# Seeding an edge-weight bank in the step that frees it, and making the edge weights one step earlier

## The chip, the core and the metric

The kernel runs on one core of a Trainium2 chip. The core has five engines that run side by side, each through its own list of instructions in order: TensorE does matrix products (PE in the profile; its weight loads are listed apart as PEld), VectorE (DVE) and ScalarE (ACT) do elementwise work, GpSimd (POOL) issues the gathers here, and SyncE (SP) issues plain DMA transfers. Engines wait for each other through semaphores. PSUM is the memory that TensorE writes its products to; it has eight banks, and VectorE and ScalarE read and write it too. The metric is the time of one execution on the device in microseconds (us); lower is better.

## What is computed

A graph network with three layers over 6250 nodes and 100000 edges, 256 features wide, and a layer norm at the end. Edges come sorted by destination.

```python
ew = edge_attr @ edge_w + edge_b                  # one weight row of 256 for each edge
for l in range(3):
    msg = relu(x[src] * ew)
    out = 0
    for i in range(3):                            # three types of edge
        h = segment_sum(msg * rel_masks[i][:, None], dst, n)
        out = out + (h * inv_cnt[i][:, None]) @ weights[l, i]
    x = x + relu(out + x @ roots[l] + biases[l])
out = layernorm(x0 + x)
```

The weights `ew` don't depend on the layer, but at 100000 x 256 numbers they are too large to keep, so each layer makes them again.

## The kernel before

Edges are cut into 391 pairs of 128-edge tiles, 256 edges a pair; two pairs are a quad. A layer takes the pairs in a fixed order: pairs 64 to 390 first, then pairs 63 down to 0. So at place p of the order the first pair of a quad stands at an even p up to place 326, and at an odd p after it. (Pair 390 is alone in its quad.)

Everything inside a layer is laid out by hand in a loop over steps `it`, one pair a step. An engine runs its instructions in the order in which this loop writes them down, so the loop is the schedule; nothing reorders it. For a quad whose first pair has place p, the steps before were:

- step p-9 and p-8, `gather`: GpSimd issues two indirect DMA transfers a pair (L989), which bring rows x[src] into `xs`; there are eight such quad buffers. SyncE loads the edge attributes `at` of eight pairs at once, nine steps ahead.
- step p-6, `seed_ew` (L611): ScalarE copies the bias `seed` into two PSUM banks `ew_p`, one for each pair. There are four such banks, so a quad uses those of the quad two before it (place p-4).
- step p-5, `make_ew` (L624): TensorE adds edge_attr @ edge_w onto the bias in these banks. In each layer the first four pairs get their bias from a small product (L620) instead of the seed.
- step p-3, `weigh`: VectorE multiplies bank and gathered rows (L646, once for each pair), ScalarE applies the relu to the quad (L648).
- step p-2, `one_hot` (L654): VectorE makes the matrices that say which node and type an edge belongs to.
- step p and p+1, `reduce`: TensorE sums the messages by node into a PSUM bank `h_p`, of which there are two.

A bank `h_p` serves a span: the pairs that fall into the same 40 nodes. Where edges are dense, a span has several pairs; then `reduce` takes the form of L668, and the span is `turned`: one step after its last pair ScalarE copies the bank out (`take`, L684), TensorE transposes it back (`turn`, L688), and in the step after that VectorE adds it to `acc` (`add`, L704). Where a span is a single pair, `reduce` takes the form of L676 and `add` follows in the next step. A layer has 244 spans, 57 of them turned; at places 77 to 140 all spans are turned spans of two pairs, which open at an odd place and close at the even place after it. From place 141 to 326 every span is one pair.

Between these steps lies the work on nodes: each 128 nodes that are complete go through `node_mul` on TensorE (L732) and `node_end` on VectorE (L763, L766), ScalarE clears their part of `acc` (L749, L752), and `root_turn`, `root_turned`, `root_mul`, `root_keep` (L709, L713, L717, L720) make x @ roots.

Within one step the order is: gathers and loads; `reduce`; `take`; `make_ew`; `turn`; `weigh`; `seed_ew`; the root and node work; `one_hot`; `add`. In the two lines below the loop's `pair(k)` is the pair at place it+k, and `first_of` says that it is the first of its quad:

```python
            if pair(5) is not None and first_of(it + 5, 2):
                make_ew(pair(5) // 2)
```

Up to place 326, `weigh` and `make_ew` therefore fall into odd steps, and `seed_ew` and `one_hot` into even steps; an odd step weighs the quad at place it+3, makes the weights of the quad at it+5, and the even step after it seeds the quad at it+7 counted from the odd step.

Of the kernel before, what the change touches and what calls it, by code (L numbers as in the profile page):

```python
# [442 lines left out]
def ordered_path(ctx, tc, x, attr_laid, A, weights, roots, biases, edge_w, edge_b, out, src, src_i, seg, place_i, consts, x_root,  # L443
# [19 lines left out]
    order, _, moved, least, most = schedule(N, E, 1)  # L463
# [75 lines left out]
    def first_of(p, n):  # L539
        return p == 0 or order[p - 1] // n != order[p] // n  # L540
# [8 lines left out]
    def closes(u):  # L549
        p = order.index(u)  # L550
        return p == U - 1 or span_of[order[p + 1]] != span_of[u]
# [28 lines left out]
    def layer(l, r_sb, b_sb, ats, early, pools):  # L580
# [22 lines left out]
        def pairs_of(q):  # L603
            return range(min(2, U - 2 * q))

        def seed_ew(q):

            for u in range(2 * q, 2 * q + len(pairs_of(q))):
                ew_ps[u] = ew_pool.tile([P, 2, D], F32, name="ew_p")
                if len(ew_ps) > OCT:  # L610
                    nc.scalar.activation(ew_ps[u], seed, AF.Copy)  # L611

        def make_ew(q):

            n = len(pairs_of(q))
            at = ats[2 * q // GROUP][:, q % (GROUP // 2), :]
            done = seen[0]
            seen[0] += n
            for k in range(max(0, min(n, OCT - done))):
                nc.tensor.matmul(ew_ps[2 * q + k].rearrange("p i d -> p (i d)"), full_ones[:PARTS, :],  # L620
                                 bias.rearrange("p i d -> p (i d)"), start=True, stop=False)
            for k in range(n):
                half = slice(k * 2 * A, (k + 1) * 2 * A)
                nc.tensor.matmul(ew_ps[2 * q + k].rearrange("p i d -> p (i d)"), at[half, :],  # L624
                                 ew_sb[half].rearrange("p i d -> p (i d)"), start=False, stop=True,
                                 skip_group_check=done + k >= OCT)
# [16 lines left out]
        def weigh(q, pairs=None):  # L643
            pairs = pairs_of(q) if pairs is None else pairs
            for k in pairs:
                nc.vector.tensor_mul(xs[q][:, k], ew_ps[2 * q + k], xs[q][:, k])  # L646
            there = xs[q][:, pairs.start:pairs.stop]
            nc.scalar.activation(there, there, AF.Relu)  # L648
# [32 lines left out]
        def take(span):  # L681
            n = D + 1 if l == 0 else D
            h_ss[span] = edge.tile([P, D + 1], F32, name="h_s", bufs=2)
            nc.scalar.activation(h_ss[span][:WK, :n], h_ps[span].rearrange("p c w -> p (c w)")[:WK, :n], AF.Copy)  # L684
# [114 lines left out]
        for j, c in enumerate(turns_of):  # L799
            step = max(3 + int((U - 110) * (1 - (1 - j / NT) ** 0.5)), max(root_at, default=-1) + 6)  # L800
            if j >= ROOTS:
                step = max(step, starts[turns_of[j - ROOTS]] + 5)
            assert step + 8 <= starts[c]
            root_at[step] = c
        for it in range(-11, max(starts) + 8):
            def pair(k):
                return order[it + k] if 0 <= it + k < U else None
# [20 lines left out]
                reduce(pair(0))  # L828
            if pair(-1) is not None and closes(pair(-1)) and turned(span_of[pair(-1)]):
                take(span_of[pair(-1)])  # L830
            if pair(5) is not None and first_of(it + 5, 2):
                make_ew(pair(5) // 2)
            if pair(-1) is not None and closes(pair(-1)) and turned(span_of[pair(-1)]):
                turn(span_of[pair(-1)])
            if pair(3) is not None and first_of(it + 3, 2):
# [4 lines left out]

            if pair(3) is not None and pair(3) // 2 == order[-1] // 2:
                weigh(pair(3) // 2, range(pair(3) % 2, pair(3) % 2 + 1))
            if pair(6) is not None and first_of(it + 6, 2):
                seed_ew(pair(6) // 2)
            if it - 6 in root_at:
                root_keep(root_at[it - 6])
            if it in root_at:
# [31 lines left out]
    with tc.manual_schedule():  # L879
        state = (*load_root(0), {}, first_rows)  # L880
        for l in range(L):
            with ExitStack() as pools:
                state = layer(l, *state, pools)
# [12 lines left out]
OCT = 4  # L896
# [25 lines left out]
def turned(span):  # L922

    return span[0] > 0 and span[1] > span[0] + 1
# [234 lines left out]
```

## Time and profile before

| what | value |
|---|---|
| three runs | 3673.85, 3688.68, 3698.54 us; median 3688.68 |
| the profiled execution | 3671.94 us, of it 3670.1 us from the first to the last instruction |
| mean granted TensorE clock | 0.883 of full speed |
| ScalarE busy | 1560.9 us, 43% of the span |
| VectorE busy | 1921.4 us, 52% |
| GpSimd busy | 2238.7 us, 61% |

Rows of the profile have the form "line engine operation out<-in shape xcount | busy us, mean ns of one | idle time of the engine just before them, and what ended it". A row of waits reads "engine, what it was about to do <- what released it: us in total, times, longest". A row of the timeline has the start in us, the length, and in brackets how long the engine stood idle before it and who released it; "x4" means four records merged into one row. One fp32 product of TensorE leaves two records, so a `make_ew` of a quad (two products) is four. The releaser "remote" or "issue" means that the profile doesn't show one.

### The profile page before, as it was taken

What the parts mean: (1) busy time and instruction counts of PE and PEld (TensorE: products, weight loads), DVE (VectorE), ACT (ScalarE), POOL (GpSimd) and SP (SyncE); (2) the same over time, 40 slices, a digit from 0 to 9 for tenths busy, and PEclk for the clock granted to TensorE, in tenths of its full rate; (3) what the DMA queues carried; (4) which work ended last, traced back from release to release, by engine and by line L of the source; (5) the groups of instructions that cost most, each with busy time, mean ns of one, the idle gap of its engine ahead of it and who ended that gap; (6) DMA issues with size and microseconds to landing.
All of it is one profiled execution on the core that took longest, in us unless ns stands there. A gap on an engine that the chain in (4) does not pass through costs nothing.

```text
span 3670.1 us, 44965 instructions
## 1 busy us (share of the span) xinstructions
PE 2851.4 (78%) x13712; PEld 1930.1 (53%) x13712; DVE 1921.4 (52%) x5485; ACT 1560.9 (43%) x2487; POOL 2238.7 (61%) x2355
## 2 busy tenths in 40 slices
PE   4787888788887767777778888776777877878877
PEld 2455565666664534445555665453444555555545
DVE  4444455566654344445555555433455565666654
ACT  3545454455444343444334344333444444434443
POOL 5666666565566566666666666656666666666664
PEclk9889999899898878988899899878788898999987
DMA  4433333333333333333333333333333333333332
GB/s 132 121 111 117 109 109 104 95 104 100 103 106 109 96 94 97 107 99 105 101 103 103 102 106 109 104 107 100 108 104 111 113 106 114 108 110 111 106 106 70
DMA packets 173571, 387.48 MB, mean 106 GB/s; under 512 B 43450, under 2 KB 78924, under 8 KB 173324
## 3 DMA queue, kind: packets, MB, share of 16 engines
q0 software_dynamic: 112608, 307.65, 29.5%
q1 hardware_dynamic: 53136, 68.50, 5.8%
q10 hardware_dynamic: 7580, 8.37, 0.8%
q8 instruction: 115, 1.88, 0.2%
q14 instruction: 132, 1.08, 0.1%
HBM read 364.88 MB, written 19.46 MB: 105 GB/s over the span
## 4 chain that ended last, share of the span: by engine, by line
PE 52%; another core or an unknown queue 15%; issue 12%; DVE 11%; ACT 5%; DMA 2%; POOL 2%; DVEq 1%; ACTq 0%; POOLq 0%; SPq 0%
PE h_p L676 15%; PE ew_p L624 13%; PE h_p L668 9%; PE o_p L732 8%; DVE xs L646 3%; PE r_p L717 3%; DVE acc L704 2%; POOL xs L989 2%; DVE oh L654 2%; ACT ew_p L611 2%; DVE x_root L763 2%; DMA xs<-x_mid,src_io 2%; ACT xs L648 2%; PE h_p L688 1%
## 5 line engine op out<-in xcount | busy, mean ns | idle before, releaser
L989 POOL DMA_INDIRECT xs<-x_mid,src_io x1564 | 1490.2, 953 | 920.3 <-issue 656.8
L648 ACT ACTIVATE xs<-xs 128x1024 f32<-128x1024 f32 (+1 forms) x588 | 616.7, 1049 | 1365.8 <-DVE xs L646 1235.7
L676 PE MATMUL h_p<-oh,xs 128*128 128x120 f32 x5160 | 790.0, 303 | 323.9 <-DVE acc L704 227.7
L989 POOL DMA_INDIRECT xs<-in_x_dram,src_io x770 | 733.8, 953 | 472.0 <-issue 316.1
L676 PEld LDWEIGHTS h_p<-oh,xs 128*128 128x128 f32 x5160 | 709.6, 211 | 519.5 <-DVE acc L704 291.1
L646 DVE TENSOR_TENSOR xs<-ew_p,xs 128x512 f32<-128x512 f32 x1167 | 751.7, 682 | 418.1 <-remote 172.6
L624 PE MATMUL ew_p<-ew_sb,at 64*128 64x512 f32 x2346 | 772.2, 720 | 100.0 <-ACT ew_p L611 73.7
L704 DVE TENSOR_TENSOR acc<-h_p,acc 128x240 f32 (+1 forms) x732 | 326.0, 445 | 996.9 <-remote 320.9
L668 PE MATMUL h_p<-xs,oh 128*120 128x256 f32 x2088 | 622.7, 431 | 151.0 <-DVE acc L704 76.9
L611 ACT ACTIVATE ew_p<-seed 128x512 f32<-128x512 f32 x1161 | 641.6, 586 | 0.0
L668 PEld LDWEIGHTS h_p<-xs,oh 128*120 128x120 f32 x2088 | 384.2, 204 | 317.5 <-issue 145.4
L654 DVE TENSOR_SCALAR oh<-iota_w,seg_o 128x120 f32<-128x120 f32 x2346 | 515.0, 293 | 0.0
L732 PE MATMUL o_p<-w_sb,acc 128*128 128x256 f32 (+1 forms) x1716 | 469.7, 413 | 48.0 <-DVE x_root L763 34.8
L732 PEld LDWEIGHTS o_p<-w_sb,acc 128*128 128x128 f32 (+1 forms) x1716 | 330.6, 205 | 175.8 <-issue 87.3
L624 PEld LDWEIGHTS ew_p<-ew_sb,at 64*128 64x128 f32 x2346 | 211.4, 207 | 239.0 <-issue 111.2
L763 DVE SCALAR_TENSOR_TENSOR x_root<-o_p,inv,x_root 128x256 f32<-128x256 f32 (+1 forms) x429 | 206.1, 480 | 168.0 <-remote 48.7
L684 ACT ACTIVATE h_s<-h_p 120x256 f32<-120x256 f32 (+1 forms) x171 | 65.3, 382 | 460.5 <-remote 259.7
L717 PE MATMUL r_p<-r_sb,t_s 128*128 128x256 f32 x588 | 170.1, 415 | 19.7 <-issue 14.1
L658 ACT ACTIVATE oh_b<-oh 128x480 bf16<-128x480 f32 x196 | 116.3, 593 | 145.5 <-DVE oh L654 112.9
L749 ACT ACTIVATE acc<-zero_o 128x768 f32<-128x768 f32 (+1 forms) x150 | 140.7, 938 | 82.7 <-PE r_p L732 21.8
L688 PEld LDWEIGHTS h_p<-ident_o,h_s 120*128 120x128 f32 x342 | 38.9, 154 | 238.8 <-ACT h_s L684 113.9
L688 PE MATMUL h_p<-ident_o,h_s 120*128 120x120 f32 x342 | 80.1, 320 | 99.3 <-ACT h_s L684 75.9
(103 smaller groups left out, 957.1 us busy)
## 6 DMA issues: line engine op xcount, KB each, us to landing
at<-in_attr_laid_dram SPq DMA_DIRECT2D x147, 256.0 KB
xs<-x_mid,src_io POOLq DMA_INDIRECT x1564
xs<-in_x_dram,src_io POOLq DMA_INDIRECT x770
x_mid<-x_all SPq DMA_DIRECT2D x96, 128.0 KB
x_all<-in_x_dram ACTq DMA_DIRECT2D x8, 768.0 KB
x<-in_x_dram SPq DMA_DIRECT2D x48, 128.0 KB
out_dram<-x_all SPq DMA_DIRECT2D x48, 128.0 KB
w_sb<-in_L_gnn_weights_dram SPq DMA_DIRECT2D x3, 768.0 KB
```

The source lines that it names most:

```text
L611: nc.scalar.activation(ew_ps[u], seed, AF.Copy)
L624: nc.tensor.matmul(ew_ps[2 * q + k].rearrange("p i d -> p (i d)"), at[half, :], ew_sb[half].rearrange("p i d -> p (i d)"), start=False, st ...
L646: nc.vector.tensor_mul(xs[q][:, k], ew_ps[2 * q + k], xs[q][:, k])
L648: nc.scalar.activation(there, there, AF.Relu)
L654: nc.vector.tensor_scalar(ohs[q][:, t, :], iota_w, seg[:, 4 * q + t:4 * q + t + 1], None, op0=ALU.is_equal)
L668: nc.tensor.matmul(by_node[:WK, :D], ohs[u // 2][:, t, :], xs[u // 2][:, u % 2, i, :], start=(i == 0 and opens(u)), stop=(i == 1 and close ...
L676: nc.tensor.matmul(h_ps[span][:, d, :], xs[u // 2][:, u % 2, i, d * P:(d + 1) * P] if d < DC else full_ones, (ohs if d < DC else oh_bs)[u ...
L704: nc.vector.tensor_tensor(there, h_ps[span][:, :CH].rearrange("p c (r w) -> p c r w", r=R), there, op=ALU.add)
L717: nc.tensor.matmul(rs[c][:, 1, :], t_ss[c][:, d, :], r_sb[:, d, :], start=(d == 0), stop=(d == DC - 1))
L732: nc.tensor.matmul(o_p[:n, j, :], acc[:, d, r, slot:slot + n], w_sb[:, r * DC + d, :], start=(d == 0), stop=(d == DC - 1))
L763: nc.vector.scalar_tensor_tensor(root, o_p[:n, j, :], inv[:n, c, r:r + 1], root, op0=ALU.mult, op1=ALU.add)
L989: nc.gpsimd.indirect_dma_start(out=xs[:, u % 2, i, :], out_offset=None, in_=x_rows[:, :], in_offset=bass.IndirectOffsetOnAxis(ap=src_i[:, ...
```

## The change

Seeding is no longer tied to a fixed step ahead of its quad. A table `seed_at` is made before the loop. For each quad it holds the latest of two steps: p-7, and the step in which the quads that used the same banks are weighed. `seed_ew` runs in that step, behind `weigh`; `make_ew` runs in the step after it. For all but two quads of a layer both entries are the same step, p-7, so `seed_ew` moves from step p-6 to p-7 and `make_ew` from p-5 to p-6; `weigh` stays at p-3. For the two quads at places 327 and 329, where the order turns round, seeding stays at p-6 and making at p-5. No instruction is added, removed or changed in shape.

```diff
@@ -802,6 +802,11 @@
                 step = max(step, starts[turns_of[j - ROOTS]] + 5)
             assert step + 8 <= starts[c]
             root_at[step] = c
+        at_first = {u // 2: p for p, u in reversed(list(enumerate(order)))}
+        seed_at = {}
+        for q, p in at_first.items():
+            used = [order[j - OCT] // 2 for j in range(p, p + len(pairs_of(q))) if j >= OCT]
+            seed_at[max([p - 7] + [at_first[x] - 3 for x in used])] = q
         for it in range(-11, max(starts) + 8):
             def pair(k):
                 return order[it + k] if 0 <= it + k < U else None
@@ -828,8 +833,8 @@
                 reduce(pair(0))
             if pair(-1) is not None and closes(pair(-1)) and turned(span_of[pair(-1)]):
                 take(span_of[pair(-1)])
-            if pair(5) is not None and first_of(it + 5, 2):
-                make_ew(pair(5) // 2)
+            if it - 1 in seed_at:
+                make_ew(seed_at[it - 1])
             if pair(-1) is not None and closes(pair(-1)) and turned(span_of[pair(-1)]):
                 turn(span_of[pair(-1)])
             if pair(3) is not None and first_of(it + 3, 2):
@@ -840,8 +845,8 @@
 
             if pair(3) is not None and pair(3) // 2 == order[-1] // 2:
                 weigh(pair(3) // 2, range(pair(3) % 2, pair(3) % 2 + 1))
-            if pair(6) is not None and first_of(it + 6, 2):
-                seed_ew(pair(6) // 2)
+            if it in seed_at:
+                seed_ew(seed_at[it])
             if it - 6 in root_at:
                 root_keep(root_at[it - 6])
             if it in root_at:
```

On each engine the order of instructions therefore moves like this. TensorE: up to place 326 `make_ew` leaves the odd steps, where it stood between `reduce` and `turn`, for the even steps, where it stands behind `reduce` too. ScalarE: the two copies of a quad stand directly behind the relu of the quad whose banks they take, ahead of that step's other copies and clears, and no longer behind the `take` of the next step. VectorE, GpSimd and SyncE keep their order.

## The prediction

> **What bounds the kernel now.** I read the page first, then the waits, then the groups with their shapes kept apart, then the timeline of two places where TensorE stands still.
>
> ```profile
> span 3670.1 us, 44965 instructions
> PE 2851.4 (78%) x13712; PEld 1930.1 (53%) x13712; DVE 1921.4 (52%) x5485; ACT 1560.9 (43%) x2487; POOL 2238.7 (61%) x2355
> ```
>
> TensorE is the busiest engine, and it stands still for 3670.1 - 2851.4 = 819 us. No other engine comes near the span. So a change of order can only win from these 819 us, and only where it gives TensorE work in a gap. The waits say what ends the gaps:
>
> ```profile
> PE h_p L676 <- DVE acc L704: 227.7, 123, 6.8
> PE h_p L668 <- DVE acc L704: 76.9, 24, 6.3
> PE h_p L688 <- ACT h_s L684: 75.9, 31, 6.4
> PE ew_p L624 <- ACT ew_p L611: 73.7, 14, 17.6
> PE ew_p L624 <- DMA at<-in_attr_laid_dram: 5.0, 1, 5.0
> DVE xs L646 <- PE ew_p L624: 120.4, 83, 7.1
> ACT h_s L684 <- remote: 259.7, 48, 13.1
> ```
>
> The largest item is a reduce that opens a span and waits until VectorE has added the span two before it, because there are two h_p banks. `make_ew` itself waits for the seeds of ScalarE for 73.7 us, in 14 places; VectorE's weighing waits for `make_ew` for 120.4 us.
>
> **The change, part by part.** The prices:
>
> ```profile
> L676 PE MATMUL h_p<-oh,xs 128*128 128x120 f32 x5160 | 790.0, 303 | 323.9 <-DVE acc L704 227.7 <-issue 83.2 <-DVE oh L654 5.9
> L611 ACT ACTIVATE ew_p<-seed 128x512 f32<-128x512 f32 x1161 | 641.6, 586 | 0.0
> L648 ACT ACTIVATE xs<-xs 128x1024 f32<-128x1024 f32 x579 | 611.1, 1055 | 1353.8 <-DVE xs L646 1224.0 <-issue 121.9 <-DMA xs<-x_mid,src_io 3.9
> ```
>
> All instructions stay, so busy time stays; only order counts.
>
> *The stage of two-pair spans.* Here the opening reduce stands at an odd place, and before the change the odd step also holds `make_ew`, behind it. So `make_ew` stands on the wrong side of the gap:
>
> ```profile
> 1506.48 1.13 PE L624 MATMUL ew_p<-ew_sb,at 64*128 64x512 f32 x4
> 1507.54 1.12 PE L668 MATMUL h_p<-xs,oh 128*120 128x256 f32 x4
> 1510.66 1.06 ACT L648 ACTIVATE xs<-xs 128x1024 f32<-128x1024 f32 x1 [5.65 <-DVE xs L646]
> 1511.62 1.10 ACT L611 ACTIVATE ew_p<-seed 128x512 f32<-128x512 f32 x2
> 1513.60 0.41 DVE L704 TENSOR_TENSOR acc<-h_p,acc 128x240 f32 x1 [2.98 <-remote]
> 1514.07 2.06 PE L668 MATMUL h_p<-xs,oh 128*120 128x256 f32 x4 [5.40 <-DVE acc L704]
> 1516.06 2.08 PE L624 MATMUL ew_p<-ew_sb,at 64*128 64x512 f32 x4
> 1518.07 0.66 PE L688 MATMUL h_p<-ident_o,h_s 120*128 120x120 f32 x2
> ```
>
> TensorE ends the even step's reduce at 1508.66, stands still for 5.40 us until the add, reduces, and then spends 2.08 us in `make_ew`. The seeds for it were ready at 1511.62 + 1.10 = 1512.72. After the change the `make_ew` comes directly behind the reduce of 1507.54, so it runs inside the gap, and the add, the reduce and the `turn` keep their times. What is saved is one `make_ew`, 1.13 us at full speed. The `turn` loses nothing by this: before, a reduce and a `make_ew` lie between the last product of the span and its `turn`, after it a `make_ew` and a reduce. How often this happens, by the windows of the stage in the three layers (280 to 485, 1508 to 1709, 2717 to 2913 us), each with its group of reduces and its two rows of waits:
>
> ```profile
> L668 PE MATMUL h_p<-xs,oh 128*120 128x256 f32 x260 | 82.0, 441 | 23.6 <-issue 18.6 <-DVE acc L704 5.0
> PE h_p L668 <- issue: 18.6, 5, 7.8
> PE h_p L668 <- DVE acc L704: 5.0, 4, 3.7
> L668 PE MATMUL h_p<-xs,oh 128*120 128x256 f32 x260 | 70.9, 407 | 32.4 <-issue 23.0 <-DVE acc L704 9.1
> PE h_p L668 <- issue: 23.0, 8, 6.9
> PE h_p L668 <- DVE acc L704: 9.1, 3, 5.4
> L668 PE MATMUL h_p<-xs,oh 128*120 128x256 f32 x260 | 75.2, 425 | 27.6 <-issue 14.7 <-DVE acc L704 12.9
> PE h_p L668 <- issue: 14.7, 6, 5.0
> PE h_p L668 <- DVE acc L704: 12.9, 5, 5.5
> ```
>
> That is 23.6 + 32.4 + 27.6 = 83.6 us in 9 + 11 + 11 = 31 gaps, and the step that waits for a bank is the opening one. A gap can hide one `make_ew`: at most 31 x 1.13 = 35 us. A few gaps are shorter than that, so I take 0.9 each: 28 us won, between 0 and 35.
>
> The Trainium skill bears on the size of this (TensorE: Matmul & The Clock Gate, Part 1): it says that TensorE's clock falls to half after an idle window of about 3.4 us, and returns after as long a busy one. The rows above agree: behind the gap of 5.40 us a reduce takes 2.06 and a `make_ew` 2.08 us, where they take 1.12 and 1.13 before it. By that rule a `make_ew` that leaves the place behind a gap that long saves 2.08 - 1.13 = 0.95 us more; if a third of the 31 gaps are that long (an estimate), the 28 us would be 38. I leave that out.
>
> *The stage of one-pair spans.* Its gaps are the 323.9 us of L676, on which I take nothing. A reduce at place p+2 waits for the add of place p, which waits for the reduce of place p. Between the two reduces lie exactly one odd and one even remainder of a step, so exactly one `make_ew`, before and after. It only moves within the same window:
>
> ```profile
> 2201.07 1.94 PE L676 MATMUL h_p<-oh,xs 128*128 128x120 f32 x16
> 2202.94 1.13 PE L624 MATMUL ew_p<-ew_sb,at 64*128 64x512 f32 x4
> 2203.99 1.13 PE L732 MATMUL o_p<-w_sb,acc 128*128 128x256 f32 x4
> 2207.82 0.41 DVE L704 TENSOR_TENSOR acc<-h_p,acc 128x240 f32 x1 [4.58 <-remote]
> 2208.28 3.67 PE L676 MATMUL h_p<-oh,xs 128*128 128x120 f32 x16 [3.16 <-DVE acc L704]
> ```
>
> Here the gap of 3.16 us stands behind two reduces, a `make_ew` and node work; after the change the `make_ew` stands between the two reduces instead of behind them, and the gap begins and ends where it did.
>
> *Weighing earlier.* VectorE no longer waits for the `make_ew` just in front, at most the 120.4 us. That is worth something only where the add behind it is waited for: 123 + 24 = 147 gaps of TensorE against the 732 adds (three layers of 244 spans) are a fifth, 24 us; and in most of the 83 waits VectorE would go on to wait for the reduce behind that `make_ew`. I take 10, between 0 and 24.
>
> *The seeds.* ScalarE's 1161 copies of 586 ns keep their number. They lose the `take` and the clears ahead of them, and put their 1.17 us a quad ahead of `t_s` and of the clears, for which nobody waits soon. But `make_ew` now needs them one step of TensorE earlier, and everything on TensorE behind it waits too. Where `make_ew` already waits for them, 14 times, the next step's reduce used to run first and now runs after: 14 x 0.97 us (a reduce of eight records, half of the sixteen at 2201.07) = 14 us lost. Most of this lies where one layer ends and the next begins, as the waits of one such stretch, 2270 to 2540 us, show:
>
> ```profile
> PE ew_p L624 <- ACT ew_p L611: 32.6, 6, 17.6
> ```
>
> There the lower bound is 0, if what feeds the stretch sets its pace anyway. New waits of this kind are the second rival, below.
>
> *The loads.* `at` is loaded in step p-9 and now read in step p-6 instead of p-5, so it has three steps to land where it had four. TensorE waited for it once in the whole trace, for 5.0 us. Nothing in SyncE's and GpSimd's queues is moved past anything else; a gather waits for a buffer that a reduce sets free, and the reduces hardly move. Zero; if the one wait came once a layer, 15 us.
>
> Sum: -28 - 10 + 14 = -24 us against 3671.94 (the span and 1.84 us around it), so 3648. The median of the runs shown lies 3688.68 - 3671.94 = 17 us higher, and the runs spread over 25; against the median it is 3665.
>
> **The rivals.** *Gaps of all stages are filled.* If half of the waits at L676 (123 for the add alone) stand ahead of an even step's work as in the first timeline, and nothing is lost at the other half, some 62 gaps more hide 1.13 us each, 70 us, and the earlier weighing brings its 24: 3688.68 - 28 - 70 - 24 + 14 = 3581. For it speaks that VectorE's lateness has many causes; against it, that a gap at an even place loses the cover that a gap at an odd place gains.
>
> *The new wait for the seeds.* This one ends slower. `make_ew` stands one reduce behind the point where VectorE's weighing begins the chain relu, copy: 1.06 + 0.59 = 1.65 us after the weighing ends. In the first timeline it has them 1512.72 - 1508.66 = 4.06 us late, inside a gap; where there is no gap and the add that lets TensorE reduce comes directly behind the weighing, TensorE has only that add's 0.41 and the reduce's 0.97 to cover 1.65, so it stops, and any further delay on ScalarE is added in full. ScalarE is held in 48 places by a `take` that waits for long (259.7 us, 5.4 each), and the relu and seeds queue behind that `take`. The Trainium skill speaks for this rival (PSUM — Partial Sum Buffer, Engine vs sequencer instructions): ScalarE's queue is strictly first in, first out, and TensorE's products keep program order, so a reduce that is ready can't pass a `make_ew` that isn't. The 14 waits agree. If one quad in four (147 of the 588 of three layers) loses 0.68 us (1.65 less one reduce), that is 100 us; with the sum above 3688.68 - 24 + 100 = 3765. It decides from 24 / 0.68 = 35 such quads on. Against it: in most quads the weighing runs well ahead, since VectorE and ScalarE are busy for only 52% and 43%.
>
> *Nothing happens.* TensorE arrives earlier at a gap that something unseen ends ("remote", "issue"), and the change moves idle time about: 3689.
>
> **How the numbers follow.** The forecast, a small gain, has 0.42: its own range is -59 (35 + 24, nothing lost) to 0, so 3630 to 3689. All gaps filled 0.18; new waits 0.3; nothing 0.1. About 1%, 37 us, is what a measurement of this kernel can tell from no change. Faster by more than that: 0.16 of the forecast's 0.42 and the whole of the second case, 0.34. Slower: most of the third case, 0.24. Within: 0.42, from the rest. The range leaves out the better half of the second case and the worse half of the third: 3590 to 3740.
>
> **What would show it.** Right: in the same stage the idle time ahead of L668 falls from 83.6 to about 55 us, the idle time ahead of L676 stays near 324, "DVE xs <- PE ew_p" falls from 120.4 to a quarter, and "PE ew_p <- ACT ew_p" grows by some 14 us. Wrong on the fast side: L676 loses idle time too. Wrong on the slow side: `make_ew` waits for the seeds in a hundred places or more instead of 14. PE's busy time should stay within 1 or 2%, by the granted clock.

## The result, and the profile after

The changed kernel takes 3717.6 us (median of 7 runs, 3711.9 to 3725.9), the kernel before 3684.5 us (7 runs, the three above among them, 3673.9 to 3698.5). The ratio is 1.0099, with a 95% interval of 1.0080 to 1.0118: a loss of 33 us, 1%, where 24 us less than before were forecast. The profiled execution of the changed kernel took 3712.46 us, with a granted clock of 0.884 (0.883 before). The ratios here and below leave out executions that fell into a slower state; among the runs of this document these are two of the six of e4, its profiled one among them.

From the page of the changed kernel, its span, TensorE's totals and the groups that the prediction spoke of (busy us, mean ns of one | idle us just ahead of them, and what ended most of it):

```profile
span 3710.7 us, 45116 instructions
PE 2921.6 (79%) x13712; PEld 1970.6 (53%) x13712; DVE 1912.7 (52%) x5485; ACT 1564.1 (42%) x2487; POOL 2240.9 (60%) x2355
L676 PE MATMUL h_p<-oh,xs 128*128 128x120 f32 x5160 | 793.0, 303 | 304.2 <-DVE acc L704 213.6
L624 PE MATMUL ew_p<-ew_sb,at 64*128 64x512 f32 x2346 | 813.7, 720 | 127.2 <-ACT ew_p L611 81.5
L668 PE MATMUL h_p<-xs,oh 128*120 128x256 f32 x2088 | 630.5, 433 | 85.6 <-DVE acc L704 61.7
L704 DVE TENSOR_TENSOR acc<-h_p,acc 128x240 f32 (+1 forms) x732 | 325.2, 444 | 1148.7 <-issue 360.8
L688 PE MATMUL h_p<-ident_o,h_s 120*128 120x120 f32 x342 | 77.9, 314 | 133.0 <-ACT h_s L684 100.8
```

The same groups of the kernel before, from its page:

```profile
L624 PE MATMUL ew_p<-ew_sb,at 64*128 64x512 f32 x2346 | 772.2, 720 | 100.0 <-ACT ew_p L611 73.7
L704 DVE TENSOR_TENSOR acc<-h_p,acc 128x240 f32 (+1 forms) x732 | 326.0, 445 | 996.9 <-remote 320.9
L668 PE MATMUL h_p<-xs,oh 128*120 128x256 f32 x2088 | 622.7, 431 | 151.0 <-DVE acc L704 76.9
L688 PE MATMUL h_p<-ident_o,h_s 120*128 120x120 f32 x342 | 80.1, 320 | 99.3 <-ACT h_s L684 75.9
```

The gaps ahead of the reduces did shrink, by 65 us at L668 (151.0 to 85.6) and by 20 us at L676 (323.9 to 304.2). TensorE's idle time in all fell by only 30 us, though (819 to 789), and its busy time grew by 70 us. The odd item is `make_ew` (L624): the same 2346 records with the same mean of 720 ns are busy for 41.5 us longer. The busy time of a line is the time in which at least one of its instructions runs. So the same instructions run side by side less often.

The waits say why. First the changed kernel's, then three rows of the kernel before (time, number of waits, the longest):

```profile
PEld ew_p L624 <- ACT ew_p L611: 121.5, 112, 15.6
PE ew_p L624 <- ACT ew_p L611: 81.5, 26, 15.2
DVE xs L646 <- PE ew_p L624: 52.7, 30, 6.8
```

```profile
PEld ew_p L624 <- ACT ew_p L611: 81.3, 25, 18.0
PE ew_p L624 <- ACT ew_p L611: 73.7, 14, 17.6
DVE xs L646 <- PE ew_p L624: 120.4, 83, 7.1
```

The matmuls wait for the copies hardly longer than before (73.7 to 81.5 us), but their weight loads (PEld) now wait in 112 places instead of 25. (The traces of these two executions hold some 18,000 semaphore updates each, where those of e1 and e5 hold 53,000, so the counts of waits are likely too low in both.) One such place in the timeline of the changed kernel (start, length, engine, line):

```profile
1352.87 1.06 ACT L648 ACTIVATE xs<-xs 128x1024 f32<-128x1024 f32 x1 [4.50 <-issue]
1353.83 1.10 ACT L611 ACTIVATE ew_p<-seed 128x512 f32<-128x512 f32 x2
1354.46 0.29 PEld L624 LDWEIGHTS ew_p<-ew_sb,at 64*128 64x128 f32 x2 [2.29 <-ACT ew_p L611]
1354.46 1.64 PE L624 MATMUL ew_p<-ew_sb,at 64*128 64x512 f32 x4 [1.88 <-ACT ew_p L611]
1354.98 0.29 PEld L624 LDWEIGHTS ew_p<-ew_sb,at 64*128 64x128 f32 x2 [0.22 <-ACT ew_p L611]
```

The relu ends, and two copies follow it, the first ready at about 1354.4, the second at 1354.93. The first product of the quad starts at 1354.46, the second at 1354.98, with the second copy. The two use different halves of the array's rows, and when both banks are ready they start together and are done after 1.13 us; here they take 1.64. The wait for the second copy counts as busy time, because the first product is still running. That is the reason why the row "PE <- ACT" hardly shows it. The start times alone, which need no semaphore, say how often this happens: of the 583 quads that stand by themselves in the records, the second product starts over 0.15 us behind the first in 27 before the change and in 118 after it, by 14.4 and 58.5 us in all.

A ledger makes the parts add up: TensorE's matmuls are taken in order of their starts, and each is charged the time by which its end lies beyond the latest end so far, the idle time ahead of it included. The sum is the time from TensorE's first to its last matmul. In us, worked out from the records of the two traces:

| group | before | after | difference |
|---|---|---|---|
| `make_ew` (L624) | 832.9 | 904.9 | +72.0 |
| reduces (L668, L671, L676) | 1839.5 | 1768.5 | -71.0 |
| `turn` (L688, L690) | 183.3 | 209.0 | +25.7 |
| root work (L709, L717) | 244.9 | 248.9 | +4.0 |
| node work (L732, L736) | 507.6 | 515.9 | +8.3 |
| the rest | 42.5 | 44.1 | +1.6 |
| sum | 3650.7 | 3691.3 | +40.6 |

What the reduces gained, `make_ew` lost, and `turn` and the rest made it a loss. Of the 72 us of `make_ew`, 44 are second products that start late (58.5 less 14.4). The other 28 are mostly idle time ahead of L624 (100.0 to 127.2 us); how much of that only stood ahead of the reduces before, these two traces don't tell.

### The profile page after: what moved, and what is told of

Same layout as the page of the kernel before. It is cut to its first block, busy times and chain, and to the rows that moved or that the text cites. A ratio compares the mean times of both kernels' runs of the same rounds, so it can differ in the third digit from the quotient of the medians.

```text
span 3710.7 us, 45116 instructions
## 1 busy us (share of the span) xinstructions
PE 2921.6 (79%) x13712; PEld 1970.6 (53%) x13712; DVE 1912.7 (52%) x5485; ACT 1564.1 (42%) x2487; POOL 2240.9 (60%) x2355
## 5 line engine op out<-in xcount | busy, mean ns | idle before, releaser
L676 PE MATMUL h_p<-oh,xs 128*128 128x120 f32 x5160 | 793.0, 303 | 304.2 <-DVE acc L704 213.6
L676 PEld LDWEIGHTS h_p<-oh,xs 128*128 128x128 f32 x5160 | 711.5, 211 | 518.7 <-DVE acc L704 280.9
L704 DVE TENSOR_TENSOR acc<-h_p,acc 128x240 f32 (+1 forms) x732 | 325.2, 444 | 1148.7 <-issue 360.8
L624 PE MATMUL ew_p<-ew_sb,at 64*128 64x512 f32 x2346 | 813.7, 720 | 127.2 <-ACT ew_p L611 81.5
L668 PE MATMUL h_p<-xs,oh 128*120 128x256 f32 x2088 | 630.5, 433 | 85.6 <-DVE acc L704 61.7
L668 PEld LDWEIGHTS h_p<-xs,oh 128*120 128x120 f32 x2088 | 381.7, 203 | 305.1 <-issue 103.5
L732 PE MATMUL o_p<-w_sb,acc 128*128 128x256 f32 (+1 forms) x1716 | 475.1, 417 | 45.3 <-DVE x_root L763 42.3
L732 PEld LDWEIGHTS o_p<-w_sb,acc 128*128 128x128 f32 (+1 forms) x1716 | 333.6, 207 | 164.9 <-issue 51.6
L624 PEld LDWEIGHTS ew_p<-ew_sb,at 64*128 64x128 f32 x2346 | 238.4, 207 | 285.7 <-ACT ew_p L611 121.5
L688 PE MATMUL h_p<-ident_o,h_s 120*128 120x120 f32 x342 | 77.9, 314 | 133.0 <-ACT h_s L684 100.8
L717 PE MATMUL r_p<-r_sb,t_s 128*128 128x256 f32 x588 | 174.8, 422 | 0.0
L717 PEld LDWEIGHTS r_p<-r_sb,t_s 128*128 128x128 f32 x588 | 106.0, 201 | 119.2 <-issue 65.1
```

The lines of the kernel that those rows point to most:

```text
L668: nc.tensor.matmul(by_node[:WK, :D], ohs[u // 2][:, t, :], xs[u // 2][:, u % 2, i, :], start=(i == 0 and opens(u)), stop=(i == 1 and close ...
L676: nc.tensor.matmul(h_ps[span][:, d, :], xs[u // 2][:, u % 2, i, d * P:(d + 1) * P] if d < DC else full_ones, (ohs if d < DC else oh_bs)[u ...
L704: nc.vector.tensor_tensor(there, h_ps[span][:, :CH].rearrange("p c (r w) -> p c r w", r=R), there, op=ALU.add)
L717: nc.tensor.matmul(rs[c][:, 1, :], t_ss[c][:, d, :], r_sb[:, d, :], start=(d == 0), stop=(d == DC - 1))
L732: nc.tensor.matmul(o_p[:n, j, :], acc[:, d, r, slot:slot + n], w_sb[:, r * DC + d, :], start=(d == 0), stop=(d == DC - 1))
```

## The experiments

Theory 1: `make_ew` reaches TensorE before its copies, and waits above all for the second. Theory 2: the loss comes from where `make_ew` stands among TensorE's other work, whether or not the copies are ready. Theory 3: it comes from ScalarE, whose copies now stand ahead of other work. Theory 4 came up after e1 to e4.

One thing has to be known to read these runs. The change was measured where the kernel before takes 3685 us. Most experiments ran on chips where the same kernel takes 2984 to 2991 us, and e8 to e11 on a chip where it takes 3640 us. So each time is read against runs of the kernel before on its own chip, or against a kernel whose time was shown to be the same on several.

**e1, the copies moved alone.**

```diff
-            if it - 1 in seed_at:
-                make_ew(seed_at[it - 1])
+            if pair(5) is not None and first_of(it + 5, 2):
+                make_ew(pair(5) // 2)
```

> One half of the change alone: ScalarE copies the bias directly behind the relu that follows the freeing weighing, as in the changed kernel, but make_ew stays at place p-5, as before the change. Theory 1 (the changed kernel loses because make_ew reaches TensorE before the second seed, so that its second product waits and no longer runs beside the first): make_ew has a whole step more of cover, so the busy time of L624 goes back from 813.7 to about 770 us, the weight loads that wait for a seed go from 112 places back to 25 or fewer, and the time is 3675 to 3690 us. Theory 2 (the loss comes from where make_ew stands among TensorE's own work, with no regard to the seeds): also about 3685. Theory 3 (the loss comes from ScalarE, whose copies now stand ahead of other work): 3710 to 3720 us, as the changed kernel.

**e2, the changed kernel with the copies ahead of the relu** (in `weigh`; `seeds` is `seed_at.get(it)`).

```diff
             there = xs[q][:, pairs.start:pairs.stop]
+            if seeds is not None:
+                seed_ew(seeds)
             nc.scalar.activation(there, there, AF.Relu)
```

> The changed kernel, but within the weighing's step the two copies of the bias are queued on ScalarE ahead of the relu instead of behind it: they come 1.06 us earlier, and the relu 1.17 us later. make_ew stays at place p-6. Theory 1 (late second seed): most of the lost overlap comes back, L624 is busy for 770 to 790 us, weight loads wait for a seed in 30 to 60 places, and since the gain ahead of the reduces (85 us) stays, the time is 3660 to 3690 us. Theory 2 (place of make_ew on TensorE): no difference to the changed kernel, 3710 to 3720 us. Theory 3 (ScalarE's order): the relu is later still, 3715 to 3740 us.

**e3, that and `turn` at the end of its step** (its two lines moved from behind `make_ew` to just ahead of `one_hot`).

> As the run with the copies ahead of the relu, and besides turn is queued on TensorE at the end of its step, behind root and node work, instead of directly behind the reduce. This asks for the idle time that moved to turn (L688 99.3 to 133.0 us). Theory 1: seeds and turn are separate items, so the idle time ahead of L688 falls by some 20 us beside the gain of the other run, 3645 to 3680 us in all. Theory 2: only the place on TensorE counts, so this alone moves the time, 3690 to 3710 us. If the steps in question hold no root or node work, turn gains nothing and the time is that of the other run.

**e4, the kernel before with the two products of a quad apart.**

```diff
-                make_ew(pair(5) // 2)
+                make_ew(pair(5) // 2, 0)
+            if pair(4) is not None and first_of(it + 4, 2):
+                make_ew(pair(4) // 2, 1)
```

> The kernel before, with one thing undone: the second product of each make_ew is queued one step later, behind the next reduce, so that the two products of a quad never run side by side. All else as before. It measures what the overlap is worth. Theory 1 says that a pair of products side by side takes 1.13 us and one alone about as long, so the busy time of L624 goes from 772 to some 1200 to 1300 us, the time to 4000 to 4200 us. If the products do not run side by side at all (the records only look so), the busy time of L624 stays near 780 us and the time within 1% of the kernel before.

e1, e2 and e3 took 2989.0, 2990.3 and 2991.0 us, with ratios of 0.9994 (0.9985 to 1.0003), 1.0000 (0.9991 to 1.0009) and 0.9998 (0.9989 to 1.0007) to the kernel before, which took 2990.5 us here. No theory had expected the three to be equal. e4 took 3361.7 us (3349.2 to 3420.0), a ratio of 1.1215 (1.1198 to 1.1232). Its row of `make_ew`, on the page of an execution of 3400.0 us:

```profile
L624 PE MATMUL ew_p<-ew_sb,at 64*128 64x512 f32 x2346 | 1361.7, 662 | 10.8 <-ACT ew_p L611 5.8
```

Apart, the 588 quads of products take 2.32 us each instead of the 1.13 of a pair side by side. The overlap is real, and the price of losing it altogether is above the 1200 to 1300 us of L624 that were expected. The time came out far below the expected 4000 us, which says that on this chip TensorE has slack.

What sets the pace there? e1's page has GpSimd's gathers, its waits have the weighing:

```profile
L994 POOL DMA_INDIRECT xs<-x_mid,src_io x1564 | 1492.8, 954 | 484.8 <-issue 378.3
L994 POOL DMA_INDIRECT xs<-in_x_dram,src_io x770 | 736.4, 956 | 234.8 <-issue 181.8
```

```profile
POOL xs L994 <- issue: 560.1, 1837, 0.3
DVE xs L646 <- DMA xs<-x_mid,src_io: 419.6, 282, 4.8
```

A gather takes 0.95 us of GpSimd and the next follows after 0.3 us; the two rows with the idle time ahead of them make 1492.8 + 736.4 + 484.8 + 234.8 = 2949 of the 2988 us. No wait of GpSimd for its own issue is longer than 0.3 us, and the weighing waits 282 times for a gather to land. Where the change was measured, such a wait of GpSimd could last 18.3 us, and by the records of the transfers, worked out by place in the queue, some nine landed pairs lay ready when a pair was weighed (median, its own among them), against one and a half in e1. The Trainium skill (Perfetto Trace Analysis, Optimizing DMA Performance) says that a kernel can be bound by the engine that issues its transfers, whose track is then full of them; these rows agree. That became Theory 4, and e5 to e7 asked for it.

**e5, the changed kernel itself.**

> The changed kernel as it is, beside runs of the kernel before taken with it, because the experiments so far ran where the kernel before takes 2990 us instead of 3685, and GpSimd issues a gather every 1.25 us there (2346 of them make 2940 us). If that place or one like it serves again: Theory 1 (late second seed, paid by TensorE wherever the kernel runs): ratio 1.006 to 1.012. Theory 4 (where GpSimd's gathers set the pace, what TensorE waits for its seeds is hidden): ratio 0.997 to 1.003, with L624 busy for longer all the same, 30 us or more above the kernel with the copies alone moved (711.2 us). If the kernel before takes 3685 us again, both expect 1.008 to 1.012.

**e6 and e7, the kernel before and the changed one with half of the gathers left out.** The second 128 rows of a pair are read in order, by SyncE:

```diff
-    for i in range(2):
+    nc.sync.dma_start(xs[:, u % 2, 1, :], x[u % 40 * 128:u % 40 * 128 + 128, :])
+    for i in range(1):
         nc.gpsimd.indirect_dma_start(
```

> The kernel before with half of the gathers left out: of the two gathers of a pair only the first is made by GpSimd, the second half of the rows comes as a plain load of 128 rows in a row of x, queued on SyncE. The output is not that of the reference. GpSimd then needs 1173 x 1.25 = 1470 us. Theory 4: where the gathers set the pace (kernel before 2990 us), TensorE becomes the bound, 2700 to 2900 us. If the gathers do not set the pace, the time stays within 1%.

> The changed kernel with the same half of the gathers left out, to be held against the kernel before with the same half left out. Theory 1: with TensorE as the bound the lost overlap is paid in full, L624 is busy for 30 to 60 us longer and the time is 20 to 50 us longer. Theory 2 (place of make_ew among TensorE's work): also longer, but with L624 busy for the same time. If the gaps that make_ew fills are worth more than what the second seed costs, the time is shorter by 10 us or more.

e5 took 2985.2 us beside 2985.4 of the kernel before, a ratio of 1.0000 (0.9991 to 1.0009). Its page shows that the loss at `make_ew` is there all the same, only hidden: it is busy for 72 us longer than in e1, where it stands at its old place. (No trace of the kernel before was taken on such a chip with all gathers.) The row of e5, then that of e1:

```profile
L624 PE MATMUL ew_p<-ew_sb,at 64*128 64x512 f32 x2346 | 783.6, 662 | 126.6 <-ACT ew_p L611 118.4
```

```profile
L624 PE MATMUL ew_p<-ew_sb,at 64*128 64x512 f32 x2346 | 711.2, 657 | 72.3 <-ACT ew_p L611 67.9
```

In e2 and e3 the copies still come late more often than Theory 1 had expected: `make_ew` is busy for 752.3 and 740.5 us there, and its weight loads wait for a copy in 167 and 153 places (30 to 60 expected; e1 122, where 25 or fewer were expected; e5 338). With `turn` at the end of its step the idle time ahead of it is 3.6 us in e3, against 7.3 in e2, so there was little to win by that on these chips.

With half of the gathers e6 took 2597.7 us (2594.5 to 2600.0), less than the 2700 to 2900 that Theory 4 had expected, and 13% less than with all: on these chips the gathers do set the pace. e7 took 2675.0 us (2672.0 to 2678.8): the change costs 77 us, 3.0%, once TensorE sets the pace. That is Theory 1 or 2, and more than the 20 to 50 us that Theory 1 had expected. TensorE's totals and `make_ew`, first on e6's page, then on e7's:

```profile
PE 2481.6 (96%) x13712; PEld 1740.2 (67%) x13712; DVE 1913.6 (74%) x5485; ACT 1561.4 (60%) x2487; POOL 1118.5 (43%) x1182
L624 PE MATMUL ew_p<-ew_sb,at 64*128 64x512 f32 x2346 | 674.9, 647 | 20.1 <-ACT ew_p L611 16.2
```

```profile
PE 2536.7 (95%) x13712; PEld 1767.5 (66%) x13712; DVE 1897.7 (71%) x5485; ACT 1562.6 (58%) x2487; POOL 1118.3 (42%) x1182
L624 PE MATMUL ew_p<-ew_sb,at 64*128 64x512 f32 x2346 | 706.0, 648 | 31.1 <-ACT ew_p L611 24.6
```

`make_ew` has 31 us more of busy and 11 us more of idle time: 42 of the 77 us. The rest is elsewhere, so the next four runs, all with half of the gathers, took the change apart.

**e8, of the change only the copies; e9, the whole change with the copies ahead of the relu** (the edits of e1 and e2).

> With half of the gathers left out, as in the two runs above (2598 us for the kernel before, 2675 us for the changed one), and of the change only the half in which the copies move: directly behind the relu, make_ew at place p-5 as before. Theory 1 (the 77 us are make_ew's wait for the copies): 2590 to 2605 us, L624 busy for 670 to 680 us. Theory 2 (place of make_ew on TensorE): the same. Theory 3 (the copies stand in the way of ScalarE's other work): 2650 us or more.

> With half of the gathers left out: the changed kernel, but the copies are queued ahead of the relu of their step. make_ew stays at place p-6. Theory 1: 2595 to 2625 us, L624 is busy for 675 to 690 us. Theory 2: 2660 to 2690 us, for make_ew stands where it stood. Mixed (the copies account for the 44 us of L624, the place for the other 34): 2625 to 2645 us.

**e10 and e11, the kernel before and the changed one without the copies**, so without the bias of the edge weights.

```diff
-                if len(ew_ps) > OCT:
-                    nc.scalar.activation(ew_ps[u], seed, AF.Copy)
...
-                                 ew_sb[half].rearrange("p i d -> p (i d)"), start=False, stop=True,
+                                 ew_sb[half].rearrange("p i d -> p (i d)"), start=done + k >= OCT, stop=True,
```

> With half of the gathers left out, the kernel before without the copies of the bias: the edge weights lack their bias, and make_ew's products start their banks afresh, so they wait for the weighing that frees the bank and for nothing of ScalarE. All theories: 2570 to 2600 us, since the copies are seldom waited for here (33 weight loads, 27.4 us).

> With half of the gathers left out, the changed kernel without the copies of the bias, to be held against the kernel before without them. Theory 1: the difference of 77 us goes down to 10 us or less, on either side, since make_ew waits for no copy. Theory 2: 60 us or more of it stays, since the order of the work on TensorE is that of the changed kernel. Mixed: some 34 us stay.

e8 took 2624.2 us, e9 2623.2, e10 2585.7 and e11 2619.5 (each within 10 us from lowest to highest). e8 lies between what Theories 1 and 2 (2590 to 2605) and Theory 3 (2650 or more) had expected, and e9 at the upper end of Theory 1's range, 25 us above e6. Without the copies the change costs 33.8 us (2585.7 to 2619.5): the case "mixed". The rows of `make_ew` in e9 and in e11:

```profile
L624 PE MATMUL ew_p<-ew_sb,at 64*128 64x512 f32 x2346 | 675.2, 645 | 13.1 <-issue 7.3
```

```profile
L622 PE MATMUL ew_p<-ew_sb,at 64*128 64x512 f32 x2346 | 673.1, 646 | 18.5 <-DVE xs L644 9.4
```

With the copies out of the way, or 1.06 us earlier, the products of a quad run side by side again (675.2 and 673.1 us, where e6 has 674.9 and e7 706.0). By their start times, the second product is over 0.15 us late in 8 quads of e6, 70 of e7, 11 of e9 and 9 of e11. That settles the share of Theory 1 where TensorE sets the pace.

Left were e8, 27 us slower than e6 though nothing on TensorE is moved in it, and whether the chip matters, for these four ran where the kernel before takes 3640 us.

**e12 to e14: e1, e2 and e6 again, to find a chip of the slower kind for the first two, and as a control.**

> The copies of the bias moved alone, make_ew at place p-5, with all gathers, once more. If the kernel before takes 3640 to 3690 us here: Theory 1 (make_ew comes too early for the copies): ratio 0.995 to 1.002. Theory 3 (the copies stand in the way of ScalarE's other work): 1.005 to 1.012. If it takes 2985 to 2990 us: 0.998 to 1.001, as in the first run of this kernel.

> The changed kernel with the copies queued ahead of the relu, with all gathers, once more. If the kernel before takes 3640 to 3690 us here: Theory 1 (late copies): the 44 us by which L624 is busy for longer come back, ratio 0.990 to 1.000. Theory 2 (place of make_ew on TensorE): 1.006 to 1.012, as the changed kernel. If it takes 2985 to 2990 us: 0.998 to 1.002, as in the first run of this kernel.

> The kernel before with half of the gathers left out, once more, as the control of the runs without half of the gathers. If the place where it runs does not matter without them: 2592 to 2604 us (2598 in the first run). If the place matters: 2615 us or more where the kernel before takes 3640 us.

**e15 and e16: e8 and e2 again.**

> Half of the gathers left out, the copies moved alone, once more (2624 us where the kernel before takes 3640 us). If the place of the run is not the reason and Theory 3 holds for this part (the copies, placed directly behind the relu, hold up ScalarE's t_s and take): 2618 to 2630 us in a place where the kernel before takes 2985 us. If the place was the reason: 2592 to 2604 us there, as the kernel before with half of the gathers left out.

> The changed kernel with the copies queued ahead of the relu, with all gathers. If the kernel before takes 3640 to 3690 us here: Theory 1 (late copies): ratio 0.990 to 1.000. Theory 2 (place of make_ew on TensorE): 1.006 to 1.012, as the changed kernel. If it takes 2985 us, this says nothing new: 0.998 to 1.002.

The chips of these runs were of the faster kind (2983.6 and 2991.4 us). e12, e13 and e16 have ratios of 0.9998 (0.9989 to 1.0007), 1.0003 (0.9994 to 1.0012) and 1.0000 (0.9991 to 1.0009) and tell nothing new. e14 took 2597.1 us, as e6. e15 took 2619.7 us, where e8 took 2624.2: the chip matters little without half of the gathers, and the copies moved alone do cost 22 to 27 us. The rows of `root_mul` and `turn` in e14, and then in e15, by groups of TensorE:

```profile
L717 PE MATMUL r_p<-r_sb,t_s 128*128 128x256 f32 x588 | 154.6, 385 | 0.0
L688 PE MATMUL h_p<-ident_o,h_s 120*128 120x120 f32 x342 | 71.9, 292 | 4.6 <-ACT h_s L684 4.6
```

```profile
L717 PE MATMUL r_p<-r_sb,t_s 128*128 128x256 f32 x588 | 157.5, 390 | 5.2 <-ACT t_s L713 4.0
L688 PE MATMUL h_p<-ident_o,h_s 120*128 120x120 f32 x342 | 72.0, 292 | 10.3 <-ACT h_s L684 10.1
```

Both wait for what ScalarE makes, `t_s` and `h_s`. The Trainium skill (PSUM — Partial Sum Buffer, Engine vs sequencer instructions) says that ScalarE's queue is strictly first in, first out, so what stands behind two copies of 0.58 us waits for both. The row of e17 below agrees: with `t_s` ahead of the copies nothing is waited for at `root_mul`. e17 moved the copies behind `t_s`.

**e17, the copies moved alone, but to the end of the weighing's step; e18, e2 a last time.**

```diff
-            if it in seed_at:
-                seed_ew(seed_at[it])
...
+            if it in seed_at:
+                seed_ew(seed_at[it])
             if pair(2) is not None and first_of(it + 2, 2):
                 one_hot(pair(2) // 2)
```

> Half of the gathers left out, the copies moved alone into the weighing's step (make_ew at place p-5), but queued on ScalarE at the end of that step, behind t_s and the clears, instead of directly behind the relu. If the 22 us of the copies moved alone come from t_s that stands behind them: the idle time ahead of root_mul (5.2 us) and the 7.8 us by which its own time grew go away, 2600 to 2610 us. If ScalarE's order is not the reason: 2616 to 2626 us, as before.

> The changed kernel with the copies queued ahead of the relu, with all gathers. If the kernel before takes 3640 to 3690 us here: Theory 1 (late copies): ratio 0.990 to 1.000. Theory 2 (place of make_ew on TensorE): 1.006 to 1.012. If it takes 2985 us: 0.998 to 1.002, and the question stays open.

e17 took 2597.4 us (2593.3 to 2602.0), the time of e6 and e14 and less than the 2600 to 2610 expected: Theory 3 holds for the copies moved alone, and all of its cost is their place ahead of `t_s`, the clears and what else ScalarE does in that step. e18 came on a chip of the faster kind again (ratio 1.0005, 0.9996 to 1.0014). The row of `root_mul` in e17:

```profile
L717 PE MATMUL r_p<-r_sb,t_s 128*128 128x256 f32 x588 | 154.5, 385 | 0.0
```

All runs with half of the gathers in the ledger of the result (us; the kernels before and after, the copies moved alone behind the relu and at the step's end, the change with the copies ahead of the relu, and the two without copies):

| group | e6 before | e7 after | e15 copies | e17 copies, end | e9 ahead | e10 before, none | e11 after, none |
|---|---|---|---|---|---|---|---|
| `make_ew` | 654.5 | 698.7 | 648.8 | 651.5 | 648.1 | 650.6 | 651.1 |
| reduces | 1209.6 | 1232.2 | 1211.9 | 1209.4 | 1232.9 | 1205.2 | 1228.8 |
| `turn` | 75.6 | 61.3 | 82.8 | 80.9 | 61.4 | 76.2 | 62.4 |
| root work | 176.9 | 198.0 | 189.6 | 176.6 | 198.0 | 176.7 | 197.5 |
| node work | 418.9 | 422.5 | 419.1 | 419.2 | 419.8 | 419.1 | 418.7 |
| sum with the rest | 2576.3 | 2654.2 | 2593.2 | 2579.6 | 2600.5 | 2566.1 | 2596.2 |
| median of the runs | 2597.7 | 2675.0 | 2619.7 | 2597.4 | 2623.2 | 2585.7 | 2619.5 |

From e6 to e7 `make_ew` loses 44.2 us; from e10 to e11, where there are no copies, 0.5. All other groups move alike in the two comparisons: reduces +22.6 and +23.6, root work +21.1 and +20.8, `turn` -14.3 and -13.8. So the 77 us are two things. The late copies cost 44 us, all at `make_ew`, and the place of `make_ew` one step earlier costs 30 to 34 us by itself, at the work whose neighbour it was or has become. e9 has the second without the first. Theory 3 adds nothing in the whole change: root work costs the same with the copies ahead of `t_s` (198.0 in e7) and without any copies (197.5 in e11).

Why do the reduces and the root work take longer in the new order, when no copies are there to wait for? The records of e10 and e11 show it. One `root_mul` (L715 here) with what stands ahead of it on TensorE, first in e10, then in e11:

```profile
1099.45 1.03 PE L666 MATMUL h_p<-xs,oh 128*120 128x256 f32 x4
1100.10 0.84 PEld L715 LDWEIGHTS r_p<-r_sb,t_s 128*128 128x128 f32 x4
1100.31 1.03 PE L715 MATMUL r_p<-r_sb,t_s 128*128 128x256 f32 x4
```

```profile
1108.20 1.13 PE L622 MATMUL ew_p<-ew_sb,at 64*128 64x512 f32 x4
1109.25 0.73 PEld L715 LDWEIGHTS r_p<-r_sb,t_s 128*128 128x128 f32 x4 [0.76 <-ACT h_s L682]
1109.26 1.13 PE L715 MATMUL r_p<-r_sb,t_s 128*128 128x256 f32 x4
```

Behind a reduce the weight load begins 0.38 us before the reduce ends. Behind `make_ew` it begins only 0.08 us before `make_ew` ends. So it is throughout: the first weight load of other work behind `make_ew` begins 0.07 us before its end, behind anything else 0.2 to 0.4 us before (medians). In the ledger the first product of a `root_mul` costs 0.25 us behind a reduce and 0.41 us behind `make_ew`. In the old order no `root_mul` stands directly behind `make_ew`, in the new one 129 do: 21 us. Of the groups of reduces 337 stand there instead of 248, which is most of their 23 us; of the `turn`s 30 instead of 141, which is their gain of 14. So the work directly behind `make_ew` pays for it, and the change put dearer work there. Why the weight load begins late there, no run here tests; the engine named in the brackets is only inferred.

## Why the prediction was wrong

- **The term that failed is "14 x 0.97 us = 14 us lost" for the seeds.** It counted the 14 places in which TensorE already waited for them, and took it that no others would come in number. By the ledger `make_ew` lost 72 us where the change was measured, 44 of them in second products that start late, in 118 quads instead of 27. Without the copies (e11) its loss with TensorE as the bound falls from 44 to 0.5 us, so that there the copies are shown to be the cause; where the kernel before takes 3685 us the trace shows the same sign (those quads, and the weight loads that wait, 25 to 112), but the copies were not taken away there.
- **The rival was right in its mechanism**: it has `make_ew` one reduce behind a chain of relu and copy, and a hundred places or more as its sign. In the row that it named, the matmuls' own waits, there are only 26; the 112 are the weight loads'. Its price was for the first copy, and left out the add's 0.41 us that the same sentence names. What it did not see is that the second copy, some 0.5 us later, is enough to part the two products of a quad, and that this shows as busy time. The forecast's own mark, a row "PE ew_p <- ACT ew_p" that grows by some 14 us, looked nearly met (by 8).
- **In the two-pair stage the idle time ahead of the reduces fell as forecast, but the stage did not get shorter.** The windows of that stage in the changed kernel (281 to 485, 1535 to 1739 and 2737 to 2936 us), the reduces and `turn`:

```profile
L668 PE MATMUL h_p<-xs,oh 128*120 128x256 f32 x262 | 82.0, 430 | 13.5 <-DVE acc L704 10.2 <-issue 3.3
L688 PE MATMUL h_p<-ident_o,h_s 120*128 120x120 f32 x64 | 13.8, 300 | 19.6 <-ACT h_s L684 13.0 <-issue 6.5
L668 PE MATMUL h_p<-xs,oh 128*120 128x256 f32 x262 | 81.5, 441 | 24.7 <-DVE acc L704 15.8 <-issue 8.9
L688 PE MATMUL h_p<-ident_o,h_s 120*128 120x120 f32 x64 | 14.1, 307 | 17.2 <-ACT h_s L684 13.3 <-issue 3.9
L668 PE MATMUL h_p<-xs,oh 128*120 128x256 f32 x259 | 75.7, 418 | 20.3 <-DVE acc L704 20.1 <-issue 0.2
L688 PE MATMUL h_p<-ident_o,h_s 120*128 120x120 f32 x64 | 14.0, 304 | 20.5 <-ACT h_s L684 16.3 <-issue 4.2
```

  Idle ahead of L668 is 13.5 + 24.7 + 20.3 = 58.5 us, where "about 55" was forecast from 83.6. The other 40 us that L668 lost (65 in all) lie outside this stage, mostly in the long spans ahead of it, on which the prediction took nothing. That the 25 us of the stage agree with the forecast of 28 is no sign that they were won: from its first reduce to the first of the next stage, the three layers' stages took 602 us before and 607 after. By the ledger the reduces won 21 us in it, and `make_ew`, root work, node work and `turn` took 22. A gap that is filled saved nothing here, because the filling made other work dearer.
- **"The turn loses nothing" was wrong.** Before the change `make_ew` stood between the reduce and `turn` and, it seems, gave ScalarE time for `h_s`; no run tested this here. In the same stage, before the change:

```profile
L688 PE MATMUL h_p<-ident_o,h_s 120*128 120x120 f32 x64 | 14.1, 303 | 15.0 <-ACT h_s L684 12.8 <-issue 2.2
L688 PE MATMUL h_p<-ident_o,h_s 120*128 120x120 f32 x64 | 15.0, 320 | 16.3 <-ACT h_s L684 13.4 <-issue 2.9
L688 PE MATMUL h_p<-ident_o,h_s 120*128 120x120 f32 x64 | 15.6, 332 | 14.1 <-ACT h_s L684 11.6 <-issue 2.5
```

  The idle time ahead of L688 was 15.0 + 16.3 + 14.1 = 45.4 us and is 19.6 + 17.2 + 20.5 = 57.3 us now; over the whole trace it goes from 99.3 to 133.0. A gap that is filled ahead of a reduce had in part moved behind it.
- **The one-pair stage** was to stay as it was, since `make_ew` "only moves within the same window". L676 lost 20 us of idle time in the whole trace, but the stage got longer, by the start times of the same reduces from 1737 to 1768 us in the three layers: most of the loss lies here. By the ledger `make_ew` (24 us) and root work (16 us) lost in it, more than the reduces gained (7). These are two traces, and in layer 2 alone the stage got 8 us shorter.
- **The weighing** waits for `make_ew` for 52.7 us instead of 120.4, less than half, where a quarter was forecast. VectorE only waits later, at the add (996.9 to 1148.7 us); a gain of 10 us from it can't be told apart in the trace.
- **ScalarE's order**: the copies were put ahead of `t_s`, "for which nobody waits soon". e15 and e17 show that, with `make_ew` at its old place, this costs 22 us once TensorE sets the pace. In the whole change it costs nothing that shows (e7 and e11).
- **The loads** cost nothing that shows, as forecast. PE's busy time grew by 2.5% (2851.4 to 2921.6), beyond the 1 or 2% allowed for.

So the sum came out at +41 us in the profiled span instead of -24: the reduces brought 71 us, more than the 28 and 10 taken for them and the weighing, and `make_ew`, `turn` and the rest took 112, where 14 were taken. The time still lies inside the stated range of 3590 to 3740 us, on the side of the rival.

Still open is how the change with the copies ahead of the relu does where the kernel before takes 3685 us: four runs of it fell on the other kind of chip. Why the kernel before takes 2985 us on some chips and 3640 or more on others was not settled either. No version that computes the same was faster than the kernel before wherever it could be told.

## What to carry to other kernels

When a step is moved up by one place, price its inputs one by one: an operation that needs two buffers is as late as the second, and matmuls that share the array lose their overlap for it without a row of waiting that says so. Look at the waits of the weight loads, and at busy time that grows with the count and the mean unchanged. Ask what the moved step was covering where it stood (here `turn` and `t_s`), which work will stand directly behind it where it goes (here `root_mul` and more of the reduces), and whether the engine that gains sets the pace at all: on the chips where GpSimd's gathers did, a loss that is worth 77 us where TensorE sets the pace cost nothing.

## What the runs showed of the hardware

- Two products over 64 rows each, on the two halves of the array, take 1.13 us together and 2.32 us when queued apart (e4, 1361.7 us for 588 quads). When the second starts late (0.52 us in the timeline of the changed kernel), the pair takes 1.64 us, and the wait counts as busy time.
- Work over 128 rows that stands directly behind these products starts its weight load 0.07 us before they end, where behind other work it starts 0.2 to 0.4 us ahead; the first product of a `root_mul` then takes 0.41 us instead of 0.25 (e10 and e11).
- The same kernel takes 2983.6 to 2991.4 us on some chips and 3640 to 3685 us on others (each set of runs had a chip of its own, so chip and time of the run aren't told apart). With half of its gathers left out the difference is gone: the copies moved alone take 2624 us on a chip of the slower kind and 2620 us on one of the faster.
- Leaving out half of the gathers takes 2985.4 us to 2597.7: in this kernel GpSimd's issue, at some 1.25 us a gather, is the next thing to work on where the kernel takes 2985 us.
